# Attention over 3202 context rows: 24 paired chunks, one plain chunk in shared banks, two rows on VectorE

## The chip, the cores and the metric

The kernel runs on one core of a Trainium2 chip, all in float32. The metric is the device time of one execution in microseconds (us), as the median of several executions. A profiled execution gives, for every instruction, engine, line, operands, start and duration. Engines: PE (TensorE), DVE (VectorE), ACT (ScalarE), POOL (GpSimd); SP is an engine used here only to issue DMAs.

## The reference

`x` holds 4096 tokens of 512 values, the context `c` 3202 rows of 512. Cut to what matters here:

```python
h   = layernorm(x)                                   # [4096, 512]
Sim = (h @ w1)[:, None] + (c @ w2)[None, :] + (h * w3) @ c.T + b_sim   # [4096, 3202]
A   = softmax(Sim, axis=1)
hq  = A @ c                                          # [4096, 512]
bar = softmax(max(Sim, axis=1)) @ h                  # one row of 512
feats = concat([h, hq, h * hq, h * bar])             # [4096, 2048]
x = x + tanh(g_xattn) * (feats @ W_qv + b_qv)
x = x + tanh(g_ffn) * moe_ffn(layernorm(x))          # top 2 of 8 experts, capacity 1280
```

`w1`, `w2`, `w3` are the three thirds of `w_sim`. The change touches the attention (the first seven lines) alone.

## The kernel before, in words

The tokens are worked in 8 groups of 512 (`NG`, `TG`). For each group `g` the program text runs `stage_s(g)` (scores), `stage_d(g-1)` (the projection with `W_qv` of the group before), `stage_e(g)` (softmax) and `stage_v(g)` (softmax times context). After the last group come `stage_d(7)`, a small projection (L921), the routing, and the expert layers (L1150, L1310), from about 1670 us to the end. PE keeps the order in which matmuls are written, as the trace shows it; a scheduler places the instructions of each engine's own stream by priorities, and `tc.issue_after(...)` holds an instruction until another has been placed. Which instruction comes ahead of which on DVE, POOL and SP is therefore read from the built streams.

**Chunks.** The 3202 context rows are cut in two halves of 1601 (`LH`), each half in 13 chunks (`NJ`): 12 of 128 rows and one of 65 (`WJ`). Chunk j of the first half is paired with chunk j of the second, so that scores and values can be done by the Strassen-Winograd scheme: 7 products of half size in place of 8. `chain` holds the 7 products of the scores of two such pairs (`PAIRS`; the seventh has a single pair, of 65 rows), in the order pa"1", p6, p7, pb"5", pa"2", p4, pb"3". Banks of PSUM pa and pb are each used twice and opened for the second time while the first content is being added: pb"3" goes onto pb only after DVE has read pb"5" (`E` (1,1), L424). Every product of one chunk is 2 logical matmuls, and each float32 matmul is two records in the trace.

**Scores.** `stage_s(g)` (matmuls at L456) writes the scores to tiles `E`, and DVE keeps running maxima in `M`. In group 0, `build(j)` makes the Winograd sums of the keys and stores them to DRAM (`kt_d`); later groups load them. At the pair of chunks jj = 4 it calls `stage_n(g+1)`: statistics of the next group's tokens (bn_stats, and POOL's power), their product with `w1` (tile `qw`), and a round trip through DRAM (`mr_d`, then `mrb`, L285 and L286) that spreads mean and 1/deviation over the partitions. `stage_a_rest` (group 0 only, beside the third pair) multiplies group 0's tokens by `w1` (`w1b`).

**Softmax.** `stage_e(g)`: subtract the maximum (L510), exponential on ACT (L511), sums (L522) and, from group 1 on, the Winograd sums `T` of `E`. `pooled(g)` takes exp of the token maxima for `bar` and spreads them by a round trip through DRAM, `eb_d` then `ebb` (L696, L698), on POOL's DMA queue.

**Values.** `stage_v(g)` (`product`, L570): group 0 does 4 plain products (two column halves by two context halves), 512 tokens wide, 26 logical matmuls each, with the router's weights computed beside. Beside them DVE also builds what later groups need: `build_values(j)` for 13 chunks (`left_sums`: four adds L344 to L347 of 128x256 into a tile `vs`, of which there are two buffers, stored to DRAM by POOL, L348) and `build_weights(c)` for the four row blocks of `W_qv` (tiles `wc` and `wt`, L365 to L372, the latter in the same two buffers). Groups 1 to 7 do 7 Winograd products of 26 logical matmuls each. In the middle, `early` loads the next queries and `between` runs `stage_w` (finishes `qw`), `stage_a` (normalises and scales the next queries, L306, L307) and `pooled` sums. At the end of `stage_v`, PE makes row sums (L659), DVE the reciprocal `ri`, and `hqT` is multiplied into the operands of `stage_d` (L668 to L676).

```python
            def left_sums(name, w, vc, dst):
                vs = sb.tile([P, 4, 256], F32, name=f"vs{name}", tag="vs", bufs=2)
                ...
                nc.gpsimd.dma_start(dst, vs[:w])
```

Of the kernel before, what the change touches and what calls it, by code (L numbers as in the profile page):

```python
# [14 lines left out]
P = 128  # L15
# [5 lines left out]
def gated_layer(ctx, tc, x, x_t, ctxt, ctxt_t, g_xattn, g_ffn, w_sim, w_sim1, b_sim, W_qv, W_qv_t, b_qv, b_qv_c, w_router, b_router, w1, b1, w2, b2, out):  # L21
# [35 lines left out]
    w1b = const.tile([P, D], F32, name="w1b")  # L57
# [56 lines left out]
    LH = L // 2  # L114
    NJ = -(-LH // P)
    WJ = [min(P, LH - j * P) for j in range(NJ)]
    PAIRS = [list(range(j, min(j + 2, NJ))) for j in range(0, NJ, 2)]
    JH = (NJ + 1) // 2
    assert len(PAIRS[-1]) == 1
    with ExitStack() as s1:  # L120
# [10 lines left out]
        kt_d = [dram.tile([P, 7, 2, WJ[j]], F32, name=f"kt_d{j}", tag=f"kt_d{j}") for j in range(NJ)]  # L131
        KSLOT = {"1": 0, "2": 1, "7": 2, "4": 3, "5": 4, "6": 5, "3": 6}

        vs_d = [dram.tile([P, 4, JH, 256], F32, name=f"vs_d{i}", tag=f"vs_d{i}") for i in range(2)]

# [17 lines left out]
        sw1 = kv.tile([P, 1], F32, name="sw1")  # L153
        qw = kv.tile([P, NT], F32, name="qw")
# [7 lines left out]
        eb_d = [dram.tile([4, P], F32, name=f"eb_d{g}", tag=f"eb_d{g}") for g in range(NG)]  # L162

        def row_of(d):

            return d.flatten().partition_broadcast(P)

# [10 lines left out]
        def stage_a_first():  # L178
# [4 lines left out]
            for t in range(4):  # L183
                q = sb.tile([P, D], F32, name=f"q{t}", tag="q", bufs=4)
# [15 lines left out]
                if t == 2:  # L200
                    with tc.issue_after(cp.ins):
                        nc.scalar.dma_start(w1b, w_sim1.partition_broadcast(P))
                        nc.scalar.dma_start(bqv, b_qv.partition_broadcast(P))
# [3 lines left out]

        def stage_a_rest(qs):
            for t, q in enumerate(qs):
                junk = sb.tile([P, 4, P], F32, name=f"jq{t}", tag="dg").rearrange("p a b -> p (a b)")  # L210
                stt(junk, q, 1.0, w1b, ALU.mult, ALU.mult, accum_out=qw[:, t : t + 1])
            nc.vector.tensor_reduce(sw1, w1b, AX.X, ALU.add)
# [51 lines left out]
        def stage_n(g):  # L264

            mv = sm.tile([P, 4, 2], F32, name=f"mv4_{g}", tag="mv4")
            xw = sm.tile([P, 4], F32, name=f"xw{g}", tag="xw")
# [3 lines left out]
            qs = []  # L271
            for i in range(4):
                t = 4 * g + i
                q = sb.tile([P, D], F32, name=f"q{t}", tag="q", bufs=4)
                with tc.issue_after(queue[-1].ins):
                    nc.sync.dma_start(q, x[t * P : (t + 1) * P, :])
                st_ = sm.tile([P, 6], F32, name=f"st{t}", tag="st")
                nc.vector.bn_stats(st_, q)
                nc.vector.bn_aggr(mv[:, i, :], st_)
                qs.append(q)  # L280
# [7 lines left out]
            for i, q in enumerate(qs):  # L288
                junk = sb.tile([P, 4, P], F32, name=f"jq{4 * g + i}", tag="dg").rearrange("p a b -> p (a b)")
                stt(junk, q, 1.0, w1b, ALU.mult, ALU.mult, accum_out=xw[:, i : i + 1])  # L290
            return mrb, mr, xw

        def stage_w(g, mr, xw):
            stt(xw, mr[:, 0, :], sw1, xw, ALU.mult, ALU.subtract)
            stt(qw[:, 4 * g : 4 * g + 4], xw, -1.0, mr[:, 1, :], ALU.mult, ALU.mult)
# [22 lines left out]
        def build(j):  # L318

            w = WJ[j]  # L320
            kt = st.tile([P, 7, 2, w], F32, name=f"ktb{j}", tag="st")
            queue.append(nc.sync.dma_start(kt[:, 0:4].rearrange("p a b w -> p (a b) w"), ctxt_t[:, j, :, :w]))
# [8 lines left out]

        def rows_of_pair(j, name):
            w = WJ[j]
            vc = sb.tile([P, 2, D], F32, name=f"vc{name}{j}", tag="vc", bufs=2)
            for h in range(2):
                with tc.issue_after(queue[-1].ins):
                    nc.sync.dma_start(vc[:w, h, :], ctxt[h * LH + j * P : h * LH + j * P + w, :])
            return vc

        def left_sums(name, w, vc, dst):  # L340

            vs = sb.tile([P, 4, 256], F32, name=f"vs{name}", tag="vs", bufs=2)
            A11, A21, A12, A22 = (vc[:w, h, c : c + 256] for h in range(2) for c in (0, 256))
            tt(vs[:w, 0, :], A21, A22, ALU.add)  # L344
            tt(vs[:w, 1, :], vs[:w, 0, :], A11, ALU.subtract)
            tt(vs[:w, 2, :], A11, A21, ALU.subtract)
            tt(vs[:w, 3, :], A12, vs[:w, 1, :], ALU.subtract)  # L347
            nc.gpsimd.dma_start(dst, vs[:w])  # L348

        def build_values(j):  # L350

            left_sums(f"v{j}", WJ[j], rows_of_pair(j, "v"), vs_d[j // JH][: WJ[j], :, j % JH, :])
# [21 lines left out]
        def load_keys(g, j):  # L374
            kt = st.tile([P, 7, 2, WJ[j]], F32, name=f"kt{g}_{j}", tag="st")
# [3 lines left out]
        def load_values(g, p, i):  # L379

            vt = st.tile([P, JH, 256], F32, name=f"vt{g}_{p}_{i}".replace(", ", "_"), tag="st")
            js = [j for j in range(i * JH, min((i + 1) * JH, NJ))]
            full = [j for j in js if WJ[j] == P]
            n = len(full)
            if isinstance(p, tuple):
                h, c = p
                r0 = h * LH + js[0] * P
                nc.sync.dma_start(
                    vt[:, :n, :], ctxt[r0 : r0 + n * P, c : c + 256].rearrange("(c p) d -> p c d", p=P)
                )  # L390
            else:
                nc.sync.dma_start(vt[:, :n, :], vs_d[i][:, p, :n, :])
            if n < len(js):
                w = WJ[js[-1]]
                if isinstance(p, tuple):
                    nc.sync.dma_start(vt[:w, n, :], ctxt[r0 + n * P : r0 + n * P + w, c : c + 256])
                else:
                    nc.sync.dma_start(vt[:w, n, :], vs_d[i][:w, p, n, :])
            return vt

        def chain(name, prod, w, nj, done):

            def cut(a):
                return a[:w, :nj, :]

            def tmp(k):
                return cut(sb.tile([P, 2, 256], F32, name=f"{k}{name}", tag=k))
# [4 lines left out]
            with tc.issue_after(live["qp"].ins):  # L412
                nc.scalar.copy(p1, cut(pa))  # L413
# [3 lines left out]
            tt(u2, cut(p6), p1, ALU.add)  # L417
# [3 lines left out]
            tt(u3, cut(p7), u2, ALU.add)  # L421
            pb = bank(f"pb{name}")
            prod(pb, "5", True, False)
            tt(done(1, 1), cut(pb), u3, ALU.add)  # L424
            prod(pa, "2", False, True)
            nc.scalar.copy(done(0, 0), cut(pa))  # L426
            p4 = bank(f"p4{name}")
            prod(p4, "4", True, True)
            tt(done(1, 0), cut(p4), u3, ALU.add)  # L429
            prod(pb, "3", False, True)  # L430
            return tt(done(0, 1), cut(pb), u2, ALU.add)

        def stage_s(g):
# [8 lines left out]
            for jj, js in enumerate(PAIRS):  # L442
# [6 lines left out]
                w, nj = WJ[js[-1]], len(js)  # L449
                e = ee.tile([P, 2, 2, nj, 256], F32, name=f"E{g}_{jj}", tag=f"E{jj}")  # L450
                E_t.append(e)

                def prod(ps, p, start, stop):
                    for jl, j in enumerate(js):
                        for k in range(2):
                            nc.tensor.matmul(  # L456
                                ps[:w, jl, :], kts[j][:, KSLOT[p], k, :], B[p][:, k, :],
                                start=start and jl == 0 and k == 0, stop=stop and k == 1, skip_group_check=True,
                            )

                if jj == len(PAIRS) - 1:
                    tt(M[:, :, 0, :], M[:, :, 0, :], M[:, :, 1, :], ALU.max)
                e_add = chain(f"s{g}_{jj}", prod, w, nj, lambda i, j: e[:w, j, i, :, :])
# [3 lines left out]
                m = M[:w, :, :nj, :]  # L467
# [3 lines left out]
                if jj == 4 and g + 1 < NG:  # L471
                    ahead[g + 1] = stage_n(g + 1)
                if jj == 0:
                    tt(m, e[:, :, 0], e[:, :, 1], ALU.max)
                else:
                    for h in (1, 0):
                        tt(m, m, e[:w, :, h], ALU.max)  # L477
# [6 lines left out]
            nc.vector.tensor_reduce(mt, ps, AX.X, ALU.max)  # L484
            ps = ps_tr.tile([P, 4, P], F32, name=f"mbps{g}", tag="tr").rearrange("p a b -> p (a b)")
# [3 lines left out]
            stt(m, qw[:, 4 * g : 4 * g + 4], bsim, mt, ALU.add, ALU.add)  # L489
# [10 lines left out]
        def stage_e(g, first):  # L500
# [6 lines left out]
            W_ = [WJ[js[-1]] for js in PAIRS]  # L507

            def powers(e, w, m):
# [7 lines left out]
            def sums(lr, jj, SM):  # L517
                w, nj = W_[jj], len(PAIRS[jj])
                if jj == 0:
                    return  # L520
                e, s = E_t[jj][:w, lr], SM[:w, :, :nj, :]
                tt(s, E_t[0][:, lr] if jj == 1 else s, e, ALU.add)  # L522

            def close(lr, SM):

                tt(SM[:, 0], SM[:, 0], SM[:, 1], ALU.add)
                tt(mb[:, lr, :], SM[:, 0, 0, :], SM[:, 0, 1, :], ALU.add)

            if first:
                for h in range(2):  # L530
                    for jj in range(n_jj):
                        w, nj = W_[jj], len(PAIRS[jj])
                        powers(E_t[jj][:w, :, h], w, mb[:w].unsqueeze(2).to_broadcast([w, 2, nj, 256]))
            for lr in range(2):
                SM = sb.tile([P, 2, 2, 256], F32, name=f"SM{g}_{lr}", tag="M")
                for jj in range(n_jj + 1):
                    if jj < n_jj and not first:
                        w, nj = W_[jj], len(PAIRS[jj])
                        powers(
                            E_t[jj][:w, lr].rearrange("p h j t -> p (h j) t"), w,  # L540
                            mb[:w, lr, :].unsqueeze(1).to_broadcast([w, 2 * nj, 256]),
                        )
                    if jj:
                        w, nj = W_[jj - 1], len(PAIRS[jj - 1])
                        sums(lr, jj - 1, SM)
                        if lr and not first:
                            e = E_t[jj - 1][:w]
                            if jj == 1:
                                continue
                            for k in ([0, 1] if jj == 2 else [jj - 1]):  # L550
                                e, w, nj = E_t[k][: W_[k]], W_[k], len(PAIRS[k])
                                t2 = ee.tile([P, nj, 256], F32, name=f"T2{g}_{k}", tag=f"T2{k}")[:w]
# [5 lines left out]
        def stage_v(g, early, between):  # L558
# [6 lines left out]
            def product(ps, what, right, start=True, stop=True, beside=iter(())):  # L565
                for i in range(2):
                    vt = load_values(g, what, i)
# [828 lines left out]
```

## Time and profile before

| | before |
|---|---|
| time, median of 3 runs | 2682.11 us (2681.76 to 2684.42) |
| the profiled execution's own time | 2680.76 us |
| its span, granted TensorE clock | 2679.0 us, 0.993 |
| busy: PE, DVE, ACT, POOL | 2630.3, 1661.0, 462.3, 237.6 us |
| group period (first score matmul of group 2 to that of group 3) | 183.91 us |
| of that: scores, `stage_d`, values | 78.65, 25.86, 78.59 us (and 0.81 us of row sums) |
| `stage_v(0)`: first matmul to row sums | 105.20 to 211.29 us |

The span is the time between first and last instruction of the profiled execution; 1.76 us more lie around it. Stage times are differences of start times on PE's timeline. In the trace a float32 matmul of 128x256 shows 379 ns as its duration, but eight records start within 1.727 us, so that one record costs 0.216 us of PE's time.

### The profile page before, as it was taken

To read this page: it belongs to the slowest core of one execution; us is meant where nothing else is said; L and a number is where in the kernel's file an instruction comes from. 1 tells how busy PE (TensorE), PEld (TensorE's weight loads), DVE (VectorE), ACT (ScalarE), POOL (GpSimd) and SP (SyncE) were. 2 spreads that over 40 slices of the span, in tenths; PEclk is the share of its full clock that TensorE was granted. 3 is DMA by queue.
4 is the path that set the end of the run, shared out by engine and by line. 5 is a ranking of instruction groups with operands and counts; after the bars stand their busy time and mean duration, and the time that the engine had idled before them with its cause. 6 is when DMAs were issued, how large, how long until landed. Compare 5 with 4: busy or idle time off the path is not lost. (4 is left out here: it accounts for less than half of the span.)

```text
span 2679.0 us, 29957 instructions
## 1 busy us (share of the span) xinstructions
PE 2630.3 (98%) x11388; PEld 2117.3 (79%) x11388; DVE 1661.0 (62%) x3263; ACT 462.3 (17%) x788; POOL 237.6 (9%) x292
## 2 busy tenths in 40 slices
PE   8999999999999999999999996999999999999999
PEld 7658888888888888888888885777777777777776
DVE  7755855936837658559357366564647575655654
ACT  1200200201201102002011043211111111111111
POOL 0210000000001000000000056000101010101010
PEclk9999999999999999999999998999999999999999
DMA  7896756646746657566446694333323142323210
GB/s 264 247 312 207 196 193 166 215 161 178 230 150 164 240 163 209 182 169 216 157 148 200 207 376 151 136 107 106 115 75 126 64 143 96 107 87 102 75 59 20
DMA packets 184051, 436.65 MB, mean 163 GB/s; under 512 B 18616, under 2 KB 85165, under 8 KB 181858
## 3 DMA queue, kind: packets, MB, share of 16 engines
q1 hardware_dynamic: 157538, 357.48, 41.7%
q0 software_dynamic: 16624, 47.37, 5.3%
q10 hardware_dynamic: 9744, 29.87, 2.9%
q8 instruction: 90, 1.47, 0.2%
q14 instruction: 55, 0.45, 0.1%
HBM read 356.22 MB, written 85.60 MB: 165 GB/s over the span
## 5 line engine op out<-in xcount | busy, mean ns | idle before, releaser
L456 PE MATMUL pas<-Qp,kt 128*128 128x256 f32 (+1 forms) x728 | 173.7, 380 | 0.0
L1150 PE MATMUL pah<-bT,w 128*128 128x320 f32 x512 | 159.1, 433 | 0.5 <-ACT p1h L1157 0.5
L570 PE MATMUL pbv<-E,vt 128*128 128x256 f32 (+1 forms) x728 | 159.5, 379 | 0.0
L570 PEld LDWEIGHTS pbv<-E,vt 128*128 128x128 f32 (+1 forms) x728 | 138.2, 190 | 18.9
L456 PEld LDWEIGHTS pas<-Qp,kt 128*128 128x128 f32 (+1 forms) x728 | 134.9, 186 | 21.0
L511 ACT ACTIVATE E<-E 128x1024 f32<-128x1024 f32 (+1 forms) x112 | 110.7, 995 | 156.2 <-DVE E L510 154.2
L510 DVE TENSOR_TENSOR E<-E,mb 128x1024 f32<-128x1024 f32 (+1 forms) x112 | 124.7, 1137 | 12.4 <-ACT mb L497 12.4
L1150 PEld LDWEIGHTS pah<-bT,w 128*128 128x128 f32 x512 | 97.4, 191 | 39.8 <-ACT p1h L1157 1.0
L1150 PE MATMUL pao<-w,h 128*128 128x256 f32 x512 | 120.9, 379 | 0.0
L1333 POOL DMA_INDIRECT out<-acc,ti x40 | 40.9, 1022 | 862.3 <-DVE dc L1199 530.5
L921 PE MATMUL x1p<-W,q2T 128*128 128x264 f32 x512 | 116.2, 388 | 0.5 <-DVE p1d L739 0.5
L1310 PE MATMUL op<-w,h 128*128 128x512 f32 x256 | 114.8, 592 | 0.0
L1150 PEld LDWEIGHTS pao<-w,h 128*128 128x128 f32 x512 | 97.3, 190 | 20.1 <-issue 7.7
L413 ACT COPY p1s<-pas 128x512 f32<-128x512 f32 (+1 forms) x56 | 31.0, 554 | 475.5 <-issue 256.5
L477 DVE TENSOR_TENSOR M<-M,E 128x1024 f32<-128x1024 f32 (+1 forms) x96 | 109.0, 1135 | 6.4
L921 PEld LDWEIGHTS x1p<-W,q2T 128*128 128x128 f32 x512 | 96.6, 190 | 17.0 <-DVE p1d L739 0.9
L429 DVE TENSOR_TENSOR E<-p4s,u3s 128x512 f32<-128x512 f32 (+1 forms) x56 | 36.5, 652 | 110.5 <-PE p4s L456 110.5
L522 DVE TENSOR_TENSOR SM<-SM,E 128x1024 f32<-128x1024 f32 (+1 forms) x80 | 88.5, 1106 | 0.0
L426 ACT COPY E<-pas 128x512 f32<-128x512 f32 (+1 forms) x56 | 31.0, 554 | 329.7 <-PE pas L456 316.1
L456 PE MATMUL p6s<-q,kt 128*128 128x256 f32 (+1 forms) x364 | 86.6, 379 | 0.0
L456 PE MATMUL p4s<-q,kt 128*128 128x256 f32 (+1 forms) x364 | 86.6, 379 | 0.0
L456 PE MATMUL p7s<-Qp,kt 128*128 128x256 f32 (+1 forms) x364 | 86.6, 379 | 0.0
(408 smaller groups left out, 5263.0 us busy)
## 6 DMA issues: line engine op xcount, KB each, us to landing
kt<-kt_d SPq DMA_DIRECT2D x84, 896.0 KB
w<-in_w SPq DMA_DIRECT2D x32, 2048.0 KB
wp<-wt_d SPq DMA_DIRECT2D x56, 520.0 KB
vt<-vs_d SPq DMA_DIRECT2D x28, 896.0 KB
vt<-vs_d SPq DMA_DIRECT2D x28, 640.0 KB
kt_d<-ktb ACTq DMA_DIRECT2D x12, 896.0 KB
buf_d<-zero SPq DMA_DIRECT2D x80, 129.0 KB
xb<-buf_d SPq DMA_DIRECT2D x40, 258.0 KB
```

The source lines that it names most:

```text
L413: nc.scalar.copy(p1, cut(pa))
L429: tt(done(1, 0), cut(p4), u3, ALU.add)
L456: nc.tensor.matmul(ps[:w, jl, :], kts[j][:, KSLOT[p], k, :], B[p][:, k, :], start=start and jl == 0 and k == 0, stop=stop and k == 1, skip ...
L477: tt(m, m, e[:w, :, h], ALU.max)
L510: live[g]["last"] = tt(e, e, m, ALU.subtract)
L511: live[g]["exp"] = nc.scalar.activation(e, e, AF.Exp)
L522: tt(s, E_t[0][:, lr] if jj == 1 else s, e, ALU.add)
L570: mm = nc.tensor.matmul(ps[b], vt[: WJ[j], j - i * JH, b * P : (b + 1) * P], right(j), start=start and j == 0 and (b == 0 or g == 0), stop ...
L921: mm = nc.tensor.matmul(ps[:, j, :B1], qTs[g][:, c, q * P : (q + 1) * P], W1[:, c, j, :], start=(c == 0), stop=(c == DC - 1))
L1150: nc.tensor.matmul(ps, a, b, start=start and i == 0, stop=stop and i == len(A) - 1, skip_group_check=True)
L1310: nc.tensor.matmul(ps, hT[:, k, 2 * MH :], W2[:, k, :], start=(k == 0), stop=(k == KH - 1))
L1333: sc = nc.gpsimd.indirect_dma_start(out=out[:, :], out_offset=rows_of(ti, s), in_=acc[:, :], in_offset=None, bounds_check=N - 1, oob_is_er ...
```

## The change

The context is cut as 2 x 12 chunks of 128 rows (`LH` = 1536), paired as before and now in 6 equal `PAIRS`; then one plain chunk of 128 rows; then two last rows (`NR` = 2). The plain chunk's scores are 8 logical matmuls into a bank `sc`, its E tile is `Ec`, and its values ride as a thirteenth chunk in four of the seven value products, those whose banks end in one output quarter. The two last rows are not on PE: each token's product with them is taken on DVE (`times_rows`: three multiply-and-accumulate passes per tile of 128 tokens in place of one), their exponentials ride in `eb`, are spread over partitions through `eb_d` to tiles `prb`, and eight DVE operations add them to `hqT` at the end of `stage_v`. `stage_n(1)` stands in `stage_v(0)` after its first product, in place of `stage_s(0)`, and the token tiles `q` have three buffers in place of four.

```diff
-    LH = L // 2
-    NJ = -(-LH // P)
-    WJ = [min(P, LH - j * P) for j in range(NJ)]
-    PAIRS = [list(range(j, min(j + 2, NJ))) for j in range(0, NJ, 2)]
+    NJ = L // (2 * P)
+    LH = NJ * P
+    LC = 2 * LH
+    PAIRS = [[j, j + 1] for j in range(0, NJ, 2)]
...
+        def times_rows(q, dst, name):
+            for k in range(1 + NR):
+                junk = sb.tile([P, 4, P], F32, name=f"jq{name}_{k}", tag="dg").rearrange("p a b -> p (a b)")
+                stt(junk, q, 1.0, wv[:, k, :], ALU.mult, ALU.mult, accum_out=dst[:, k : k + 1])
...
+        def left_rows(g, xw):
+            tt(xw[:, :, 1:], xw[:, :, 1:], kr.unsqueeze(1).to_broadcast([P, 4, NR]), ALU.add)
+            mr_ = sm.tile([P, 4], F32, name=f"mx{g}", tag="mxr")
+            nc.vector.tensor_reduce(mr_, xw[:, :, 1:], AX.X, ALU.max)
...
         def stage_a_rest(qs):
+            w23 = sb.tile([P, 2, D], F32, name="w23", tag="vs", bufs=2)
+            with tc.issue_after(queue[-1].ins):
+                nc.sync.dma_start(w23.rearrange("p k d -> p (k d)"), w_sim_r[D:].partition_broadcast(P))
+            for r in range(NR):
+                stt(junk, wv[:, 1 + r, :], 1.0, w23[:, 0, :], ALU.mult, ALU.mult, accum_out=kr[:, r : r + 1])
+            tt(wv[:, 1:, :], wv[:, 1:, :], w23[:, 1, :].unsqueeze(1).to_broadcast([P, NR, D]), ALU.mult)
+            nc.vector.tensor_reduce(sw, wv, AX.X, ALU.add)
             for t, q in enumerate(qs):
-                stt(junk, q, 1.0, w1b, ALU.mult, ALU.mult, accum_out=qw[:, t : t + 1])
+                times_rows(q, xw[:, t, :], t)
...
         def stage_n(g):
-                q = sb.tile([P, D], F32, name=f"q{t}", tag="q", bufs=4)
+                q = sb.tile([P, D], F32, name=f"q{t}", tag="q", bufs=3)
...
-            for i, q in enumerate(qs):
-                stt(junk, q, 1.0, w1b, ALU.mult, ALU.mult, accum_out=xw[:, i : i + 1])
+                times_rows(q, xw[:, i, :], t)
...
-                if jj == 4 and g + 1 < NG:
+                if jj == 4 and 0 < g < NG - 1:
                     ahead[g + 1] = stage_n(g + 1)
...
+            ps = bank(f"sc{g}")
+            for i, terms in enumerate((((0, "1"), (1, "2")), ((2, "3"), (3, "7")))):
+                for a, p in terms:
+                    for k in range(2):
+                        nc.tensor.matmul(ps[:, i, :], kc[:, a, k, :], B[p][:, k, :], ...)
+            nc.scalar.copy(ec, ps)
+            tt(M[:, :, 0, :], M[:, :, 0, :], ec, ALU.max)
...
+            tt(mt, mt, left[g][1], ALU.max)
...
                         product(ps, (h, i * 256), ...)
+                        if (i, h) == (0, 0):
+                            with tc.issue_after(v["last"].ins):
+                                ahead[1] = stage_n(1)
...
-                product(p2b, (1, 0), right(0, 1))
+                product(p2b, (1, 0), right(0, 1), rest=rest_of(0), right_c=ec[:, 0, :])
...
-                product(pbb, 0, right(0, 0), stop=False)
+                product(pbb, 0, right(0, 0), stop=False, rest=rest_of(256), right_c=ec[:, 1, :])
...
-                product(p4b, (1, 256), right_t)
+                product(p4b, (1, 256), right_t, rest=rest_of(256), right_c=ec[:, 0, :])
...
-                product(pbb, 3, right(1, 1), start=False)
+                product(pbb, 3, right(1, 1), start=False, rest=vd_d, right_c=ec[:, 1, :])
...
+            for c in (2, 3, 0, 1):
+                for r in range(NR):
+                    stt(hqT[:, c, :], v["prb"][r], cr[:, c, r : r + 1], hqT[:, c, :], ALU.mult, ALU.add)
...
-            nc.vector.reciprocal(ri, ps[:, 0, :4])
+            tt(ri, ps[:, 0, :4], v["eb"][:, 1, :], ALU.add)
...
         def pooled(g):
-            nc.gpsimd.dma_start(eb_d[g].rearrange("i p -> p i"), eb)
+            nc.scalar.activation(eb[:, 1:, :], live[g]["xw"][:, :, 1:].rearrange("p i r -> p r i"), AF.Exp)
+            nc.gpsimd.dma_start(eb_d[g].rearrange("r i p -> p (r i)"), eb.rearrange("p r i -> p (r i)"))
...
+                for r in range(NR):
+                    nc.gpsimd.dma_start(prb[r], row_of(eb_d[g][1 + r]))
```

In the stream of POOL as it is built, group 0's `eb_d`, `ebb` and two `prb` transfers come first, then the five operations and the two transfers of `stage_n(1)` (`mr_d`, `mrb`), and after them all the stores of built values and weights; before, `mr_d` and `mrb` stood ahead of `eb_d`. In the stream of DVE, the sums of `stage_e(0)` (L522) alternate with the passes of `stage_n(1)`, the 12 value builds, one small build for the plain chunk (`vd`) and the four weight builds follow, and behind the last of them stand the last four `hqT` additions of group 0 and the first `u2`, `u3` and `E` of `stage_s(1)`.

## Prediction

> **What bounds the kernel now.** The first view is the busy time of each engine over the span:
>
> ```profile
> PE 2630.3 (98%) x11388; PEld 2117.3 (79%) x11388; DVE 1661.0 (62%) x3263; ACT 462.3 (17%) x788; POOL 237.6 (9%) x292
> ```
>
> PE is busy for 98%, DVE for 62%. An average doesn't say where each is needed, so the second view is PE's timeline at the end of the scores of group 2 (start, duration, matmuls):
>
> ```profile
> 466.89 1.89 PE L456 MATMUL pbs<-Qp,kt 128*128 128x256 f32 x8
> 468.62 1.03 PE L456 MATMUL pas<-Qp,kt 128*65 128x256 f32 x4
> 469.48 1.03 PE L456 MATMUL p6s<-q,kt 128*65 128x256 f32 x4
> 474.66 1.92 PE L724 MATMUL pad<-wp,hqT 128*128 128x260 f32 x8
> ```
>
> Starts follow each other without a gap. Eight records take 466.89 to 468.62, 1.73 us, and four of the 65-row chunk 0.86 us: a short chunk costs what a full one does, 0.216 us a record. So in groups 1 to 7 PE's count of records is the time, as long as DVE keeps up. The waits of DVE say how much room it has:
>
> ```profile
> DVE hqT L653 <- PE p4v L570: 73.8, 7, 10.5
> DVE hqT L655 <- PE pbv L570: 64.5, 7, 9.2
> ```
>
> (total, times, longest): in every values stage DVE stands idle for about 10 us ahead of each of the last products. The third view is group 0, where the chain runs through POOL and DMA. Its POOL timeline (in brackets the idle time before, and what ended it):
>
> ```profile
> 93.90 0.62 POOL L286 DMA_DIRECT2D mrb<-mr_d  x1 [12.16 <-DMA mr_d<-mr]
> ...
> 111.79 6.06 POOL L494 TENSOR_SCALAR nl<-lmax 128x1 f32<-128x1 f32 x1 [7.49 <-issue]
> ...
> 128.86 0.56 POOL L698 DMA_DIRECT2D ebb<-eb_d  x1 [9.43 <-DMA eb_d<-eb]
> 129.41 0.76 POOL L348 DMA_DIRECT2D vs_d<-vsv  x1
> ```
>
> Each small spread stops the queue for 9 to 12 us, and the first store of built values goes out only behind the last of them, at 129.41. DVE's timeline shows both ends of what hangs on these stores:
>
> ```profile
> 136.59 0.42 DVE L344 TENSOR_TENSOR vsv<-vcv 128x256 f32<-128x256 f32 x1 [3.90 <-DMA vs_d<-vsv]
> ...
> 209.01 0.42 DVE L371 TENSOR_TENSOR wt<-wc,wt 128x260 f32<-128x260 f32 x1
> ```
>
> The third build waited for the first store to land, since `vs` has two buffers; the last of 15 further builds ended at 209.4, 4.85 us for each, 2 us before `stage_v(0)` ended at 211.29. This chain has almost no room.
>
> [...]at 129.41 a store whose data was ready at 127.55 waited behind `ebb`. [...]the trace has 6.3 us for `vs_d`, which I use. [...]the first values pair at 105.20 takes 2.07 us, after a few short idle stretches, against 1.10 later.
>
> **The gain on PE.** Scores of a group g of 1 to 7: before 13 chunks x 7 products x 2 logical matmuls = 182; after 12 x 7 x 2 + 8 = 176. Values: before 7 x 26 = 182; after 7 x 24 + 4 x 2 = 176. Six logical matmuls, 12 records, less in each: 24 x 0.216 = 5.18 us a group, 36.3 us in seven. Group 0: scores 12 x 0.216 = 2.6; values 4 x 26 = 104 logical before, 4 x 24 + 2 x 2 = 100 after, 8 records x 0.43 (512 wide, 24 records from 200.99 to 211.29) = 3.4. Together 42.3 us. I take it as certain.
>
> **The seam from group 0 to group 1** is the main cost. `stage_n(1)` moves from the scores of group 0, where DVE had room, into the sums of `stage_e(0)`. With it its POOL operations and two transfers now come behind `eb_d`, `ebb`, two `prb`, and ahead of every store of values. Step by step, from rows of before: `nl` ends at about 117, first sum on DVE 120.7. Until the statistics of the fourth tile DVE does 10 sums of 1.14 us, 4 smaller ones and 9 passes, 4 bn_stats and 4 small operations: 11.4 + 1.9 + 9 x 0.68 + 4 x 0.68 + 0.7, about 22 us: 143. POOL's power and copies take 2.3: `mr_d` at 145.5. It lands 12.2 us later (as before, 4-byte elements), `mrb` goes at 158, and the first value store at 159.5, 30 us later than before. It lands at 166; `stage_a`'s first multiplication needs `mrb` (6.2 us, 165) and stands on DVE ahead of the third build. So the third build starts at about 167.5 and the 15 that remain (10 values, the plain one, 4 weights) take 4.1 (6.3 plus a share of two, with all loads ready) to 4.85 each: ends at 229 to 240, I take 231. Behind them on DVE stand four `hqT` additions (0.7 each), `qT`, `hs`, `u2`, `u3`, `E`(1,1): 2.7 + 8.3, at 242. PE: `stage_v(0)` starts at 103.9 (105.2 less 2.6, plus 1.3 from below), takes 106.1 - 3.4, row sums 0.8, so group 1 starts at 207.4 and stands at pb"3", which needs `E`(1,1), six products (10.4) and a little later, at 218.4. Stall 24 us; 8 if DVE is quicker at each step and builds take 3.6, 35 if they take 5.5.[...]
>
> **The other costs**, all on DVE or POOL; where I put nothing, the cover is named.
> - Scores of group 0: `stage_a_rest` gains ten passes, a 128x1024 product and a wider sum, some 9 us, and two broadcasts of 512 KB, where `stage_n(1)` (about 6 us) has left. PE meets `E`(1,1) of the next pair at about 68.1, DVE is there at 68.0: 1 us, 0 to 5. Row maxima: two small operations, 0.3.
> - Maxima of later groups: PE's transpose and diagonal product are placed between products of `stage_d`; one more DVE operation adds 0.25 to a chain with 0.14 room: 0.17 x 7 = 1.2, 0 to 3.
> - Start of the scores in groups 2 to 7: four `hqT` additions and two `ri` operations put 3.0 us ahead of `u2`; PE's need comes about 11.6 us after the start and DVE gets there at 11.5. Nothing, up to 1 each. Cover gone, it is 3 us a group.
> - `stage_n` in groups 1 to 6: eight more passes, 5 us, over two pairs in which DVE has about 6 us idle each. Nothing, up to 2 each.
> - `eb_d` is three times as long in 4-byte elements (estimated 15 us where 512 took 9.4). Its readers in groups 1 to 7 come at the end of the values, over 40 us later: nothing. In group 0 it is part of the above, POOL being idle until 143.
> - `stage_d(7)` follows the values directly and needs corrected `hqT`: four additions, 2.7 us, 1.5 to 5.
> - PSUM banks, `ec`, `kc_d`, `vd_d`: loads and copies beside PE, nothing; a loss of 1 at most.
>
> Sum: 42.3 - 26 - 1.3 - 1.2 - 2.7 = 11.1 us. Against the profiled execution's 2680.8 that is 2669.7; the median of the runs shown is 1.3 higher, so 2671.
>
> **Rivals.**
> 1. The seam is hidden. If the builds run at 3 us each, once all values are loaded (their adds are only 4 x 0.34 us), they end near 213 and the stall is under 5 us. For it: DVE and loads have room. Against it: 6.3 us landing and two buffers, seen to pace the stores at 4 to 5 us. Gain 42.3 - 5 - 5 = 32 to 37: about 2648.
> 2. DVE becomes the bound at every pair of scores. Place: L424 ahead of pb"3" at the start of each group, and pairs 3 and 4 with `stage_n`. Price: 3.0 us of additions and 5 us of passes are together 8 us, against 5.2 gained a group. It decides once less than 3 us of these hide: over 5.3 lost in each of six groups, with the 31 of the sum, is 63 against 42.3, 2700. For it: at the start the room is 1.8 us. Against it: 10 us waits in the values, 6 us in a pair. Half of it gives 2686.
> 3. The small spreads on POOL (`eb_d`, two `prb`, then `mr_d`) add up: if `eb_d` takes 15 and `mr_d` is held until `prb` is done, at 143 it is just free; were it held 10 us longer the seam grows by 10: 2681. That is "no change".
>
> **How the numbers follow.** The likeliest case, a seam of 12 to 37 us, has 0.60 and gives 2658 to 2683. Rival 1 has 0.20, rival 2 0.10, rival 3 0.10. About 0.2% (5.4 us) is what a measurement of this kernel can tell from no change: faster is below 2676.7, all of rival 1 and 0.9 of the main case, 0.76 with a little of the rest; same, between 2676.7 and 2687.5, 0.14; slower 0.10. The range leaves out the best end of rival 1 and most of rival 2: 2645 to 2685.
>
> **What would show it.** In the changed profile: the group period 178.7 us in groups 2 to 6; the first `vs_d` store near 159; one PE gap ahead of pb"3" in group 1, near 218, of 8 to 35 us, released by DVE `E`, and none elsewhere above 3 us. Wrong, if that gap is missing, or if each group shows one.

## The result, and the profile after

The changed kernel takes 2672.99 us (median of 7 runs, 2670.72 to 2676.28) against 2683.76 us for the kernel before (7 runs, 2681.76 to 2685.27, the three shown above among them). The ratio is 0.9962, with a 95% interval of 0.9951 to 0.9974: faster by 10.8 us. The forecast was 2671. The profiled execution is one of the slower ones, 2675.19 us with a span of 2673.4.

Busy time on the page of the changed kernel:

```profile
PE 2593.4 (97%) x11200; PEld 2096.8 (78%) x11200; DVE 1706.4 (64%) x3432; ACT 458.4 (17%) x788; POOL 241.7 (9%) x301
```

PE has 36.9 us less work. DVE has 45 us more, and it is still not the engine with the most work. PE's timeline at the end of the scores of group 2 (start, duration, matmuls):

```profile
482.84 1.89 PE L507 MATMUL pbs<-Qp,kt 128*128 128x256 f32 x8
484.57 3.62 PE L531 MATMUL sc<-Qp,kc 128*128 128x256 f32 x16
488.02 1.92 PE L820 MATMUL pad<-wp,hqT 128*128 128x260 f32 x8
```

The seven stretches of four records for the 65-row pair have become one stretch of 16 records into `sc`, and no gap is beside it. DVE's waits in the values (total, times, longest):

```profile
DVE hqT L728 <- PE p4v L639: 73.7, 7, 10.5
DVE hqT L730 <- PE pbv L639: 45.9, 7, 6.6
```

Ahead of the last product but one, DVE is as idle as before; ahead of the last, the first four additions to `hqT` have used 2.7 us of the idle time. Now POOL's timeline in group 0 (idle before, and what ended it, in brackets):

```profile
125.29 0.58 POOL L781 DMA_DIRECT2D ebb<-eb_d  x1 [9.05 <-DMA eb_d<-eb]
...
142.01 0.99 POOL L321 DMA_DIRECT2D mr_d<-mr  x1 [0.30 <-POOL mr L319]
...
152.70 0.58 POOL L322 DMA_DIRECT2D mrb<-mr_d  x1 [9.22 <-DMA mr_d<-mr]
153.28 1.51 POOL L391 DMA_DIRECT2D vs_d<-vsv  x2
```

Two stores were ready at 142.8 and 144.2 and left at 153.28, behind `mrb`. DVE's timeline shows what follows from it:

```profile
160.08 2.29 DVE L343 TENSOR_TENSOR qT<-qT,mrb 128x2048 f32<-128x2048 f32 x1 [14.39 <-DMA mrb<-mr_d]
162.28 0.42 DVE L387 TENSOR_TENSOR vsv<-vcv 128x256 f32<-128x256 f32 x1
...
229.66 0.43 DVE L422 TENSOR_TENSOR wt<-wc,wt 128x260 f32<-128x260 f32 x1
...
240.24 0.69 DVE L474 TENSOR_TENSOR E<-pbs,u3s 128x512 f32<-128x512 f32 x1
```

DVE stood for 14.39 us at the multiplication of the next queries (L343), with the third build behind it; the last of 15 builds ended at 230.1, and `E`(1,1) of group 1 could be added at 240.24. PE meanwhile:

```profile
208.99 1.89 PE L507 MATMUL p7s<-Qp,kt 128*128 128x256 f32 x8
213.76 1.97 PE L507 MATMUL pbs<-q,kt 128*128 128x256 f32 x8 [2.88 <-DVE we L679]
...
219.02 0.59 PE L507 MATMUL pas<-Qp,kt 128*128 128x256 f32 x2
240.99 3.78 PE L507 MATMUL pbs<-Qp,kt 128*128 128x256 f32 x8 [21.38 <-DVE E L474]
244.56 2.56 PE L507 MATMUL pas<-Qp,kt 128*128 128x256 f32 x6
```

Two gaps, 2.88 and 21.38 us, both ended by DVE, and after the longer one eight records take 3.57 us where they take 1.73 at 248.68, and the next six 2.40 in place of 1.30: 2.9 us more. The granted clock was 0.50 from 222.89 to 246.78 us, so for the first 5.8 us behind the restart; from 247 to 260 it was 1.00. One more gap is at the end, between the row sums of group 7 and its projection:

```profile
1484.55 0.95 PE L738 MATMUL rsps<-ones,mb 128*128 128x1 f32 x8
1487.79 3.74 PE L820 MATMUL pad<-wp,hqT 128*128 128x260 f32 x16 [2.29 <-issue]
```

Starts on PE's timeline, side by side with the steps of the forecast (us):

| | before | changed | change | forecast |
|---|---|---|---|---|
| first values matmul of group 0 | 105.20 | 102.09 | -3.1 | -1.3 |
| first scores matmul of group 1 | 212.11 | 205.45 | -6.7 | -4.7 |
| period of group 1 | 183.90 | 206.51 | +22.6 | +21.0 |
| period of group 3 | 183.91 | 178.90 | -5.01 | -5.01 |
| row sums of group 7 to `stage_d(7)` | 0.81 | 3.24 | +2.4 | +2.7 |
| first `x1p` matmul | 1524.78 | 1512.41 | -12.4 | -11.1 |
| first expert transpose (`bps`) | 1670.86 | 1663.73 | -7.1 | -11.1 |

Up to `x1p` the profile follows the forecast. Between `x1p` and the experts, in code that the change does not touch, this execution lost 5.2 us; that is taken up below.

### The profile page after: what moved, and what is told of

Its sections match the earlier page's. It is cut to its first block, busy times and chain, and to the rows that moved or that the text cites. A ratio compares the mean times of both kernels' runs of the same rounds, so it can differ in the third digit from the quotient of the medians.

```text
span 2673.4 us, 29708 instructions
## 1 busy us (share of the span) xinstructions
PE 2593.4 (97%) x11200; PEld 2096.8 (78%) x11200; DVE 1706.4 (64%) x3432; ACT 458.4 (17%) x788; POOL 241.7 (9%) x301
## 5 line engine op out<-in xcount | busy, mean ns | idle before, releaser
L507 PE MATMUL pas<-Qp,kt 128*128 128x256 f32 x672 | 161.6, 382 | 0.0
L639 PE MATMUL pbv<-E,vt 128*128 128x256 f32 x672 | 147.3, 379 | 0.0
L507 PEld LDWEIGHTS pas<-Qp,kt 128*128 128x128 f32 x672 | 128.0, 191 | 17.4
L639 PEld LDWEIGHTS pbv<-E,vt 128*128 128x128 f32 x672 | 127.7, 190 | 17.4
L580 ACT ACTIVATE E<-E 128x1024 f32<-128x1024 f32 x96 | 100.9, 1057 | 129.5 <-DVE E L579 128.6
L579 DVE TENSOR_TENSOR E<-E,mb 128x1024 f32<-128x1024 f32 x96 | 115.3, 1216 | 11.4 <-ACT mb L566 11.4
L507 PE MATMUL pbs<-Qp,kt 128*128 128x256 f32 x336 | 81.3, 386 | 21.4 <-DVE E L474 21.4
L525 DVE TENSOR_TENSOR M<-M,E 128x1024 f32<-128x1024 f32 x80 | 97.9, 1224 | 4.5
L507 PEld LDWEIGHTS pbs<-Qp,kt 128*128 128x128 f32 x336 | 64.8, 193 | 30.8 <-DVE E L474 21.8
L507 PE MATMUL pbs<-q,kt 128*128 128x256 f32 x336 | 79.4, 379 | 2.9 <-DVE we L679 2.9
```

The costliest lines, as they stand in the source:

```text
L507: nc.tensor.matmul(ps[:, jl, :], kts[j][:, KSLOT[p], k, :], B[p][:, k, :], start=start and jl == 0 and k == 0, stop=stop and k == 1, skip_ ...
L525: tt(M, M, e[:, :, h], ALU.max)
L579: live[g]["last"] = tt(e, e, m, ALU.subtract)
L580: live[g]["exp"] = nc.scalar.activation(e, e, AF.Exp)
L639: mm = nc.tensor.matmul(ps[b], vt[:, j - i * JH, b * P : (b + 1) * P], right(j) if j < NJ else right_c, start=start and j == 0 and (b == 0 ...
```

## The experiments

Theory: the stall is the end of a chain, late first store, then builds one behind the other, then `E`(1,1). It was late since POOL's queue and DVE's stream both stood behind the round trip of group 1. The rivals stand with each run. Each group of runs was measured beside the kernel before on one chip (medians of before 2683.81, 2683.32 and 2682.83 us). This table holds the measurements (us; "scores 1" is the start of group 1, "gaps" are PE's idle stretches in its first pair of chunks, "to d(7)" is from the row sums of group 7 to `stage_d(7)`):

| kernel | values 0 start | scores 1 | period 1 | gaps | to d(7) | median | ratio, 95% interval |
|---|---|---|---|---|---|---|---|
| e1 statistics in the scores | 114.39 | 217.70 | 190.56 | 6.25 + 2.08 | 3.24 | 2669.86 | 0.9944 (0.9928 to 0.9961) |
| e2 stores on ACT | 101.86 | 204.99 | 210.58 | 5.21 + 6.55 + 14.03 | 3.24 | 2679.49 | 0.9980 (0.9971 to 0.9989) |
| e3 statistics after second product | 101.57 | 204.76 | 196.05 | 4.45 + 7.63 | 3.24 | 2663.16 | 0.9917 (0.9901 to 0.9934) |
| e4 rows not added | 103.07 | 207.00 | 202.61 | 2.47 + 16.43 | 0.81 | 2665.69 | 0.9927 (0.9911 to 0.9944) |
| e5 weights in the scores | 102.69 | 206.07 | 181.44 | 1.33, and 0.66 in a later pair | 3.24 | 2652.88 | 0.9887 (0.9870 to 0.9903) |
| e6 both moved | 103.23 | 206.15 | 178.89 | none | 3.24 | 2648.93 | 0.9877 (0.9860 to 0.9893) |
| e7 double additions | 102.74 | 206.19 | 204.27 | 22.9 | 5.89 | 2677.09 | 0.9978 (0.9970 to 0.9987) |
| e8 changed again | 102.12 | 204.84 | 204.23 | 2.2 + 21.2 | 3.23 | 2674.94 | 0.9962 (0.9951 to 0.9973) |
| e9 rows added early | 102.55 | 205.70 | 180.24 | 1.07 in a later pair | 0.81 | 2643.33 | 0.9854 (0.9838 to 0.9871) |
| e10 before, weights moved | 104.76 | 210.86 | 186.54 | 2.37 in a later pair | 0.81 | 2689.07 | 1.0023 (1.0014 to 1.0031) |

**e1: `stage_n(1)` back in the scores of group 0.**

```diff
-                if jj == 4 and 0 < g < NG - 1:
+                if jj == 4 and g < NG - 1:
...
-                        if (i, h) == (0, 0):
-                            with tc.issue_after(v["last"].ins):
-                                ahead[1] = stage_n(1)
```

> stage_n(1) goes back into stage_s(0), all else as changed. Theory (the seam's stall is a late first store: POOL's queue and DVE's stream both stand behind the round trip mr_d/mrb of group 1, and from the third value build on two buffers pace the builds): the round trip is over before eb_d, the first value store goes at about 128 to 134, the builds end near 208, the gap ahead of pb"3" of group 1 falls from 21 us to 0 to 4. The scores of group 0 get 12 DVE passes more and lose 3 to 8 us. Time 2648 to 2656. Rival 1 (the stall is the amount of DVE work behind the values of group 0: four hqT additions, a 13th build, the passes): the gap stays above 10 us, time over 2662. Rival 2 (loads or DRAM traffic pace the builds): gap stays above 15 us.

The gap at pb"3" fell to 2.08 as the theory has it, but pb"5" waited 6.25 us for DVE, and the scores of group 0 lost 12.3 us and not 3 to 8. PE's timeline of this kernel at the end of those scores:

```profile
96.15 3.78 PE L531 MATMUL sc<-Qp,kcb 128*128 128x256 f32 x8 [4.42 <-DVE kcb L372]
99.78 3.06 PE L507 MATMUL pbs<-Qp,ktb 128*128 128x256 f32 x8
106.47 1.12 PE L546 MATMUL mps<-ident,M 128*128 128x128 f32 x4 [3.64 <-DVE M L541]
```

DVE came late with the sum of the plain chunk's keys (`kcb`) and with the maxima, and part of what PE did here was slow: the eight records at 96.15 take 3.63 us, eight at 86.39 took 1.72. The granted clock was 0.92 on average from 12 to 114 us, in the changed kernel 0.99 from 12 to 102. So the first store went at 148.65, 4.6 us earlier than in the changed kernel, not 20. The builds still ended at about 229, and PE arrived 12 us later, which is most of why its gaps are smaller. In this place the statistics cost 12.3 us of the scores, and yet the kernel is not slower than the changed one (ratio 0.9944, 0.9928 to 0.9961, against 0.9962): what the scores lose, the seam gives back. Whether the theory of the seam holds can't be read from this run; its time was missed by 14 us.

**e2: the value stores from ACT's queue.**

```diff
-            nc.gpsimd.dma_start(dst, vs)
+            nc.scalar.dma_start(dst, vs)
```

> Only the queue of the 12 value stores changes, from POOL's to ACT's; stage_n(1) stays in stage_v(0). Theory: the first store goes at 143 in place of 153, yet the third build still starts near 160 to 162, since on DVE it stands behind the multiplication of the next queries (L343), which waits for mrb. The gap ahead of pb"3" falls by 0 to 6 us, time 2666 to 2673. Rival (POOL's queue alone is the cause): third build near 150, the gap falls by 10 us or more, time below 2664.

The first store left at 142.56, 10.7 us earlier. The third build did not move forward:

```profile
163.81 2.29 DVE L343 TENSOR_TENSOR qT<-qT,mrb 128x2048 f32<-128x2048 f32 x1 [18.35 <-DMA mrb<-mr_d]
166.02 0.42 DVE L387 TENSOR_TENSOR vsv<-vcv 128x256 f32<-128x256 f32 x1
```

So POOL's queue alone is not the cause: DVE waits for `mrb` whichever queue takes the stores (18.35 us here, 14.39 in the changed kernel). The two stores now left right behind `mr_d` (142.56 and 141.78), and `mrb` left at 157.84 in place of 152.70; that they delayed it was not shown. The time was missed, though (2679.5 for 2666 to 2673): the copies that ACT makes for group 1 (`hqT`, then `p1s`) stood in its queue behind four stores, which left one by one between 206.69 and 223.48, each as its late build was done, and PE waited 6.55 us for `p1s`. It is a new wait in place of the one removed: the three gaps are 25.8 us together, against 24.3.

**e3: `stage_n(1)` behind the second product.**

```diff
-                        if (i, h) == (0, 0):
-                            with tc.issue_after(v["last"].ins):
-                                ahead[1] = stage_n(1)
...
+                        if (i, h) == (0, 1):
+                            with tc.issue_after(v["last"].ins):
+                                ahead[1] = stage_n(1)
```

> stage_n(1) stays in stage_v(0) but is written after its second product and that product's builds, so that on POOL six value stores and two weight stores stand ahead of mr_d and mrb. Theory: first store near 127, third build near 132, builds end at 205 to 212, gap ahead of pb"3" of group 1 0 to 6 us, no loss in the scores of group 0: 2645 to 2654. Rival 1 (amount of DVE work): the passes are still there, gap stays above 10 us, time over 2660. A new wait is possible: the next queries' operands come too late for the first product of group 1; then a gap at the start of group 1 instead.

First store 119.70, third build 129.06, 33 us ahead of the changed kernel, and the gaps halved (24.3 to 12.1). Not all of the 33 us are the move's: POOL's `nl` (L563), a small operation ahead of `eb_d`, showed 0.49 us here and 6.41 in the changed kernel. It differs in the same way between e6 (0.41) and e9 (7.40), which share their code up to this point and whose first stores lie 6 us apart. The last build ended at about 219, 11 us sooner and not some 20, so the time lies outside its range and in that of rival 1, the amount of DVE's work; e5 and e6 decide between them. POOL's timeline says why:

```profile
162.54 0.98 POOL L321 DMA_DIRECT2D mr_d<-mr  x1 [0.29 <-POOL mr L319]
...
175.41 0.59 POOL L322 DMA_DIRECT2D mrb<-mr_d  x1 [11.64 <-DMA mr_d<-mr]
176.00 0.76 POOL L391 DMA_DIRECT2D vs_d<-vsv  x1
184.12 0.71 POOL L391 DMA_DIRECT2D vs_d<-vsv  x1 [7.36 <-DVE vsv L390]
```

The round trip had moved into the middle of the stores and held them there. And DVE waited for loads as well (4.90 and 6.31 us for `vcv`). A late first store is one part of the chain; its length is the other. e3 alone does not show that it is the larger one.

**e4: the last rows' additions and their maximum left out.**

```diff
-            tt(mt, mt, left[g][1], ALU.max)
...
-            for c in (2, 3, 0, 1):
+            for c in ():
```

> Left out: the eight additions of the last two rows to hqT in every group, and their maximum (mt); all their products and exponentials stay. Theory: stage_d(7) starts 2.3 us sooner, the group period falls from 178.90 to 178.73, the gap ahead of pb"3" of group 1 falls by the four additions behind the last build, 2.7 us: together 6 us, time 2667 (2665 to 2669). Rival (the additions hold each start of scores up): period falls by more than 0.5 us, time below 2664.

`stage_d(7)` starts 0.81 us behind the row sums again, and the period of groups 3 to 5 is 178.71 in place of 178.90 (groups 2 and 6 have 179.41 and 179.15, with short waits of PE in the values). Period 1 is 1.6 to 3.9 us shorter than in the two profiles of the changed kernel, around the 2.7 of the four additions; from the end of the last build to that of `E`(1,1) DVE takes 8.5 us in place of 10.8. With 2665.7 it lies inside its range.

**e5: the four weight builds in the scores of group 1.**

```diff
+                if g == 1 and jj < DC:
+                    with tc.issue_after(e_add.ins):
+                        build_weights(jj)
...
-                            for c in [[], [0, 1], [2], [3]][2 * i + h]:
-                                build_weights(c)
```

> The four weight builds (wc, wt) leave stage_v(0) and are written into stage_s(1), one behind each of its first four pairs; stage_n(1) stays where the change put it. Theory (the seam is a chain of builds at 4.5 us each that ends before E(1,1) of group 1 can be added): four builds of 15 less behind the third, the chain ends 15 to 18 us sooner, near 213, the gaps at pb"5" and pb"3" of group 1 fall from 24 us together to 6 to 10, and the scores of group 1 hide the builds moved there. Time 2654 to 2660. Rival (the round trip of mr_d alone sets it, the builds ride along): gaps stay above 18 us, time over 2666.

2652.88 us. `mr_d` and `mrb` left at 142.60 and 152.92 as in the changed kernel, so the round trip is as late as it was; only the chain behind it is shorter. DVE's timeline of this kernel:

```profile
206.93 0.43 DVE L402 TENSOR_TENSOR vd<-vcr 128x256 f32<-128x256 f32 x1 [2.42 <-DMA vs_d<-vsv]
...
217.70 0.69 DVE L474 TENSOR_TENSOR E<-pbs,u3s 128x512 f32<-128x512 f32 x1
```

The last build ends at 207.4 in place of 230.1, `E`(1,1) comes at 217.70 in place of 240.24, and the gap is 1.33 us. So the length of the build chain ahead of `E`(1,1) is enough to make the stall, with the round trip as late as before. Four builds were worth 22.7 us here, 5.7 each, where 4.5 was put; hence the time just below its range. DVE's own work on them is only 7.5 us of it. In the changed kernel DVE stands idle, between the third build and the last, 21.7 us for stores that must land to free a buffer and 11.3 us for loads from DRAM; in e5 these are 16.1 and 1.2 us. So the loads, rival 2 of e1, pace the chain as well as the two buffers do.

**e6: both moves, e3 and e5 together.**

> stage_n(1) behind the second product of stage_v(0), as in the third experiment, and the four weight builds in stage_s(1). Theory: both parts of the chain are shortened, the value builds end near 203, the gaps of group 1 fall to 0 to 3 us[...], so that nearly all of the gain in matmuls is seen: 2645 to 2652. Rival (the copy of the router's bank, or the next queries' operands, come late instead): a gap of more than 4 us stays at the start of group 1, time over 2653.

2648.93 us. PE starts group 1 at 206.15 without a gap, the value builds end at 195, and the period of group 1, 178.89, is that of every other group. The passes, the `hqT` additions and the 13th build are all still there, so rival 1 of e1 and e3, the amount of DVE's work behind the values, falls.

**e7: each addition to `hqT` twice.**

```diff
-                for r in range(NR):
-                    stt(hqT[:, c, :], ...)
+                for r in [r for r in range(NR) for _ in range(2)]:
+                    stt(hqT[:, c, :], ...)
```

> Each of the eight additions of the last rows to hqT is made twice (the output has these terms doubled); all else as changed. Theory: at the start of groups 3 to 7 DVE ends E(1,1) 0.74 us ahead of pb"3" in the changed kernel; four additions more (2.7 us) turn that into a stall of 2.0 us in each of groups 2 to 7, with 2.7 us more at the seam and ahead of stage_d(7): 17 us, 2690 (2686 to 2694). Rival (other slack hides them, as it hid the first four): only the seam and the last stage pay, 5.4 us, 2678.

The theory was wrong and the rival nearer: the period of groups 2 to 6 stayed at 178.90, and the median is 2.2 us above e8's. That is the last stage alone; the seam, from which the rival too took 2.7 us, paid nothing (`E`(1,1) ended at 239.63, in e8 at 239.47). The PE timeline of the start of group 3, of this kernel, has the reason:

```profile
598.07 1.89 PE L507 MATMUL p4s<-q,kt 128*128 128x256 f32 x8
599.80 1.89 PE L507 MATMUL pas<-Qp,kt 128*128 128x256 f32 x8
601.53 1.89 PE L507 MATMUL p6s<-q,kt 128*128 128x256 f32 x8
603.25 0.59 PE L507 MATMUL p7s<-Qp,kt 128*128 128x256 f32 x2
603.68 1.89 PE L507 MATMUL pbs<-Qp,kt 128*128 128x256 f32 x8
```

Between p4 and pb"3" stand 18 records of the next pair. The changed kernel has six at this place, and e4, without the additions, none. Here is the same pb"3" in the changed kernel, whose group 3 starts at 590.87, and then in e4, where it starts at 589.02:

```profile
602.60 1.89 PE L507 MATMUL pbs<-Qp,kt 128*128 128x256 f32 x8
```

```profile
599.46 1.89 PE L507 MATMUL pbs<-Qp,kt 128*128 128x256 f32 x8
```

So pb"3" comes 10.4, 11.7 and 14.3 us after the start of the group as DVE has none, four or eight additions ahead of `E`(1,1), though the program text writes it directly behind p4 in all three. PE's matmuls do not keep the order of the text, which was said above of the kernel before; in these three the built order follows DVE's work. DVE ended that addition at 603.0. Room read from one built order (0.74 us) is not the room there is: an edit that makes DVE longer also gets another order. The last stage, which has nothing else to put in between, paid the 2.65 us in full (5.89 for 3.24).

**e8: the changed kernel again.**

> The changed kernel once more, beside the others on one chip: 2671 to 2675. Open is the stretch from the first x1p matmul to the experts, 154.0 us in its first profile and 148.7 in that of before, in code that the change does not touch. If it varies from run to run, this profile may show 149; if it is a cost of the change, it shows 154 again.

2674.94 us. The stretch from `x1p` to the experts' first transpose was 152.62 us, so it was long again (151.32 in the first profile, 146.09 before; the 154.0 and 148.7 of the expectation end 2.7 us later, at the next transposes). In both profiles of the changed kernel, and in those of e3 and e5 (150.21, 151.06), ACT stood once for 4.6 to 5.6 us; in the other eight profiles, that of before among them, no such wait is there, and the stretch is 146.1 to 147.6. ACT's waits in that stretch, changed kernel:

```profile
ACT xn L1135 <- DMA w<-in_w: 4.6, 1, 4.6
```

ACT issues the stores of `out` there: a store whose data DVE had written by 1550.9 left at 1556.08. The profile names the landing of the experts' weight loads `w` as what ended the wait; the tokens behind it came late and PE waited (2.49 us at 1567.27, for DVE). e1, e2, e6 and e7 hold the same code here and do not show it, so it is not a fixed cost of the change. The runs of the kernels here spread by 2.6 us (e4) to 11 us (e2), those of before by about 7, and the wait is of a like size; that the wait is the cause of the spread was not tried.

**e9: the rows' terms added ahead of the last product.** From e6:

```diff
+                for half, q in ((hqT[:, 0:2, 0:256], 0), (u2, 256)):
+                    for c in (0, 1):
+                        for r in range(NR):
+                            stt(half[:, c, :], v["prb"][r][:, q : q + 256], cr[:, c, r : r + 1], half[:, c, :], ALU.mult, ALU.add)
                 product(pbb, 3, right(1, 1), start=False, rest=vd_d, right_c=ec[:, 1, :])
...
-            for c in (2, 3, 0, 1):
+            for c in (2, 3) if g else (2, 3, 0, 1):
```

> As the sixth experiment (stage_n(1) behind the second product, weight builds in stage_s(1)), and in groups 1 to 7 the last rows' terms of the first two column blocks are added before the last value product, one half to hqT, the other to u2, so that no addition stands behind that product. Theory: the gap of 3.24 us from the row sums of group 7 to stage_d(7) closes to about 0.8,[...] and nothing else changes: 2649 less 2.4 to 5, so 2644 to 2647. Rival (the gap is set by the rest of the chain, hqT, qT, hs, not by the additions): 2649.

2643.33 us, a little below the range and the fastest kernel of the study: the gap ahead of `stage_d(7)` is closed (0.81), and the first 16 records there take 3.6 us, where they took 5.3 in e6. In this profile a later pair of group 1 has a gap of 1.07 us that e6's has not. Against before it gains 39.5 of the 42.3 us that the matmuls were put at.

**e10: the weight builds moved in the kernel before.**

> The kernel before with its four weight builds moved into stage_s(1) and nothing else. Theory: the chain of builds ended 2 us ahead of the end of stage_v(0) before, and PE had no gap at the start of group 1, so shortening it gives nothing: within 3 us of before. Rival (the builds cost PE time as such, by traffic or DVE load): faster by 5 us or more.

2689.07 us, not faster but 6 us slower than before (1.0023, 1.0014 to 1.0031), so the theory's 3 us were missed too. The rival falls: nothing was gained by taking the builds from where they stood. In the scores of group 1 they cost a gap of 2.37 us at pb"3" of a later pair, released by DVE's `E`. The profiled execution, 2684.53 us, is one of the faster of the 14, so the rest of the 6 us stays open. So the move is no gain of its own. In e5 it gave back what the change had put there.

## Why the prediction was right, point by point

- **The gain on PE.** The periods of groups 2 to 6 fell by 5.01 us, the 5.18 of 12 records less the 0.17 that was put for the maxima. That term is shown too: `stage_d`, where the maxima's matmuls stand, takes 26.06 us in place of 25.86; without the extra maximum (e4) it takes 25.87, with the additions doubled (e7) 26.07. Its working does not come out, though: 0.25 us added to a chain with 0.14 of room gives 0.11. The values of group 0 fell by 3.5 us (3.4). e9, with most costs gone, gains 39.5 us of the 42.3 in all.
- **The seam.** First store 153.3 (forecast 159.5), third build 162.3 (167.5), last build ended at 230.1 (231), `E`(1,1) ready at 240.9 (242), PE at pb"3" at 219.5 (218.4), gaps 24.3 us (24), and 2.9 us lost behind them at a granted clock of 0.50 (2). That the end was met within 1 us is in part luck. The chain began 5.2 us sooner than forecast: `mr_d` left at 142.01 (145.5), and `mrb` 10.7 us behind it (12.5). And each build took 4.5 us where the likely case had 4.2. The upper price of the stall does not follow from its working: 15 builds at 5.5 us end at 250, which makes it 43 us and not 35. The shape was off as well: part of the stall was taken at pb"5", which needs the PSUM bank that held the router's products. DVE's copy out of it (`we`, L679) stands among the late builds. The forecast named one gap. The sum's 26 us are the stall's 24 and 2 more for a slower PE behind it, which was the author's estimate: before shows a slow pair at 105.20, with the granted clock at 0.50 from 99.90 on, but no stall of this length.
- **What was right for a reason that is only half the reason.** The forecast put most weight on the place of the statistics. e3 and e5 divide it: moving them alone halves the gaps (12 us), shortening the chain by four builds alone nearly closes them (1.3 us). PE ended `stage_v(0)` 6.7 us sooner with 15 builds still to do from the third on, where before the chain had ended with 2 us to spare. DVE's `E`(1,1) and PE's pb"3" of group 1 in the kernel before:

```profile
219.61 0.69 DVE L424 TENSOR_TENSOR E<-pbs,u3s 128x512 f32<-128x512 f32 x1
```

```profile
222.55 1.89 PE L456 MATMUL pbs<-Qp,kt 128*128 128x256 f32 x8
```

The addition ended 2.25 us ahead of the matmul that needs it. So a values stage that is 6.7 us shorter would probably not have been cashed in full even with the chain as it was; no run tests that alone.
- **Scores of group 0.** A loss of 1 us was put for `stage_a_rest`; there was none, the first values matmul came 0.5 us earlier than the count of records gives. The one gap of before at this place (1.97) became 1.71 and 0.23. What left, `stage_n(1)`, paid for what came; e1, which brings it back, shows 12 us.
- **Start of groups 2 to 7.** No stall, as put, with 0.74 us of room. e7 shows that the cover is the order in which PE's matmuls are built, and that rival 2 was further off than its price said. The eight further passes of `stage_n` are hidden too: they stand in groups 1 to 6, and the period is 178.90 in each of groups 2 to 6.
- **`stage_d(7)`.** 2.43 us (2.7), shown by e4 and e9. In six other profiles with this gap (e1, e2, e3, e5, e6, e8) the first 16 records behind it also took 5.3 us (6.6 in e5); in the first profile of the changed kernel they took 3.6, at a granted clock of 1.00.
- **Rivals 1 and 3.** Builds at 3 us each did not come: they took 4.5. `eb_d` with its 1536 elements held POOL's queue 10.4 us in group 0, as 512 elements did before, and not the estimated 15; `mr_d` left 0.3 us after its data was ready, so nothing added up there.
- **Not foreseen.** 5.2 us between `x1p` and the experts in the profiled execution. The total was right on the medians (10.8 us of gain for 11.1), which the sum was not made for. Between the two profiled executions, for which it was made, the gain is 5.6 us: the sum up to `x1p` was 1.3 us too small, the stretch described under e8 took back 5.2, and the experts behind it, in code that is the same, another 1.6.

## What to carry to other kernels

When the busiest engine gets less to do in one stage, look at who shares that stage: a chain of builds and stores that ended just in time before can end too late (2.25 us to spare before, 24.3 us of gaps after), and part of the gain is lost in gaps at the next stage. Count what hangs on a slow round trip (`mr_d` to `mrb`, 10.7 us) on every queue it passes, the issuing engine's and the reader's; moving the stores off one of them (e2) gained nothing. And where such a chain is late, work with a later deadline (here the weight builds, needed only by `stage_d(0)`) can go behind the seam: that was worth 22 us in e5, and cost 6 us in e10, where the chain was not late.

## What the runs showed of the hardware

In four of twelve profiles ACT stood once for 4.6 to 5.6 us at the stores of `out`, with weight loads under way; why only there is open. In e2 its copies came 6.55 us late behind stores that waited for their builds.

POOL's first `nl`, a 128x1 operation, showed 0.26 to 0.49 us in e1, e3 and e6, and 6.06 to 7.40 in before, the changed kernel, e2 and e9, and moved the transfers behind it by nearly as much (`eb_d` left at 108.62 in e6 and at 115.36 in e9). A store of 1536 single elements (`eb_d` of the changed kernel) took 10.4 to 13.2 us from its issue to that of its reader, one of 512 (before) 9.1 to 11.3: three times as many cost on average 1.4 us more.

Behind a gap of 2.3 us, with only eight one-column matmuls (0.8 us) ahead of it, the first 16 records of `stage_d(7)` took 5.3 to 6.6 us in six profiles, and 3.6 in the first of the changed kernel, where the granted clock was 1.00; why they differ is open. In before the granted clock was 0.50 from 99.90 to 110.14, behind two idle stretches of 1.5 us, the second not yet over; the first values pair, at 105.20, took 2.07 us, later ones 1.10.
